# A bidirectional scan layer on one core: a main loop of hand-written order against four ordered lists, with half of a small product replaced

## The chip, the cores and the metric

The kernel runs on one core of a Trainium2 chip. The metric is device time in microseconds of that core; lower is better. The engines are called as the profile calls them: PE (TensorE, matrix products; PEld is its weight load), DVE (VectorE), ACT (ScalarE), POOL (GpSimd) and SP (SyncE, which here only issues DMAs). Each engine takes its instructions in order and waits on semaphores for the others. PE writes to PSUM, which has eight banks of 512 f32 columns on 128 partitions; POOL does not touch PSUM in this kernel.

## What is computed

Four images of 128 channels by 96 x 96 are normalised in groups, read as sequences in four directions (rows, rows reversed, columns, columns reversed), each run through the same small recurrent layer, and fused back into the image. Cut to what matters, with `x` a sequence of length 9216:

```python
t = grouped1x1(x, in_proj_w, in_proj_b, 4)          # 128 -> 512 channels
u, gate = t[:, :256], t[:, 256:]
u = depthwise_conv(silu(u), dw_w)                   # 5 taps along the sequence
s = ssm_in_w @ u                                    # 32 channels
a = clip(0.999 + 0.0009 * sigmoid(delta_w @ u + delta_b))
b, c = tanh(b_w @ u + b_b), tanh(c_w @ u + c_b)
h = scan(h' = a * h + b * s)                        # written with cumulative sums in the reference
u = u + ssm_out_w @ (c * h + d * s)
y = out_proj_w @ grouped1x1(u * sigmoid(gate), mix_w, mix_b, 4) + out_proj_b
out = x + sum over the directions of fuse_w[direction] @ y + fuse_b
```

Everything is f32.

## The kernel before, in words

The sequence is cut into steps of 16 image lines (6 steps for a pass), and a step's 1536 positions into four residues modulo 4, `p` = 0 to 3, so that a tile has 384 columns. A forward sequence and its reverse are handled together as `s` = 0 and 1: one **pair** is one residue of one step for both. There are 4 images x 2 orders (columns "V", rows "H") x 6 steps x 4 residues = 192 pairs; 24 pairs make a phase (one image, one order). In the second half of a phase the two sequences have met: the data of a step are those of a mirrored earlier step, so its silu values and gates are not computed again but loaded back from DRAM, where they had been stored (`kept_sil`, `kept`).

For each pair the work is, with the names of the tiles:

- **front** (first half of a phase only, four pairs ahead): input projection `psum<-x_in,wn` on PE (L134), silu on ACT (L481) into `sil`. Channels 0 to 127 (block 0) are laid out so that partitions hold 32 channels of four neighbouring residues, channels 128 to 255 (block 1) one residue each.
- **convolution**: block 1 by five taps, the first on ACT (L624), four on DVE (L626), the last of which writes `u`. Block 0 on PE: a product with the banded matrix `band` (128 rows, 8 matmuls) in `conv`, and in `conv_less` one with a half-band matrix `less` (64 rows, 8 matmuls) for the taps that reach into the neighbouring group of four residues. ACT copies the sum to `u` (L607, L609).
- **projections** `psum<-u,main` (16 matmuls), tanh and copies on ACT (L655 to L657, L669), decay and b*s on POOL (L659, L660).
- **scan** on DVE (L686), in two halves once in four pairs, and on POOL c*h, + d*s and a copy (L692 to L694).
- **gates**: `psum<-x_in,wn` from four matmuls (L492) and four tanh on ACT (L515), first half only.
- **state out** `psum<-t,main` (L498, four matmuls), added to `u` by an earlier copy of `u` into the bank on ACT (L506, `under`), or by a DVE add (L574) where the pair is one of the first; then the gating on DVE (L575).
- **result** `psum<-u,w_fin` (16 matmuls), copied by ACT (L717, L719) and added to the image `acc` in SBUF by POOL (L733). After the last pairs of an image `acc` is stored to `out` and reloaded with the next image.
- for the V order, statistics of the next image by `bn_stats` on DVE (L398).

A matmul of f32 shows as two entries in the profile, so the 16 matmuls of a projection are "x32".

What sets the order: `pair(t)` emits all of this for slot `t`, engine by engine in the order of its statements, with the later stages of the pair `t - 6` (`LAG`). The scheduler is off (`manual_schedule`), so each engine's queue is this order. Banks are fixed by hand (`SSM`, `TAPS`, `PROJ`, `FRONT`, `GATE`). `late` postpones the adds of an image's first pairs until its reload; `tail` drains the last six pairs, with half of the adds on DVE. All loads and stores are issued by SP in the same order.

Of the kernel before, what the change touches and what calls it, by code (L numbers as in the profile page):

```python
# [61 lines left out]
LAG = 6  # L62
UB = 8
NP = NS * R


@with_exitstack
def conv_preact_kernel(
# [28 lines left out]
    for ph, (b, order, dirs) in enumerate(phases):  # L97
        for st in range(NS):
            for p in range(R):
                for s in range(2):  # L100
# [10 lines left out]
                            "k": 2 * p + s,  # L111
# [9 lines left out]
    SSM, TAPS, PROJ = 0, 0, (4, 5)  # L121
    FRONT = (7, 6, 2, 3)
    GATE = {True: (6, 4, 5, 7), False: (4, 7, 6, 5)}

    def plan(with_front):

        return (PROJ, FRONT[:2]) if with_front else (FRONT[:2], PROJ)

# [40 lines left out]
    stats, free = {}, [FRONT[1]]  # L169
# [134 lines left out]
    d_sb, b_mix, b_out, b_fuse = (w_small[:, a:b] for a, b in ((79, 80), (80, 82), (82, 83), (83, 84)))  # L304
    w_out = w_out_fuse[:, 0:HID]
# [21 lines left out]
    less = wp.tile([P, R, 4, 32], F32, name="less")  # L327
# [8 lines left out]
    for s in range(2):  # L336
        for p in range(R):
            for k in range(2):
                r, to = slice(0, P), band[:, s, p]
                if k == less_of(p):  # L340
                    r, to = less_rows(s, p), less[:, p]
# [41 lines left out]
    def chunks_of(t):  # L383

        un = units[2 * t]
        b, k = un["b"] + 1, t % R
        if un["order"] == "V" and b < B and k > 1:
            return [(b, un["st"] * R + 2 * (k - 2) + e) for e in range(2)]
        return []

    def load_chunks(t):
        for b, c in chunks_of(t):
            chunks[b, c] = wk.tile([P, SC], F32, tag="xs", name=f"xs_{b}_{c}")
            nc.sync.dma_start(chunks[b, c], xr[b, :, bass.ts(c, SC)])

    def stats_chunks(t):
        for b, c in chunks_of(t):
            nc.vector.bn_stats(stats_of(b)[:, c, :], chunks.pop((b, c)))  # L398


    sils = {}
# [3 lines left out]
            [  # L405
                dp.tile([P, 2, 2, N + 1], F32, tag=f"sil{e}_{st}_{g}", name=f"sil{e}_{st}_{g}")
                for g in range(R)
            ]
            for st in range(NS // 2 - 1)
# [4 lines left out]
    def front(i, banks):  # L414
        for _ in front_parts(i, banks):
            pass

    def front_parts(i, banks):

        step, g = divmod(i, R)  # L420
        if step * UB >= NU:
# [7 lines left out]
        elif g == 0 and fresh(step):  # L429
            sils[step] = wk.tile([P, 2, 2, 4, N + 1], F32, tag="sil", name=f"sil_{step}")  # L430
        if fresh(step):
            yield from compute_front(step, g, banks)
        sil = sils[step]

        if st == 0:
            engine = nc.gpsimd if step else nc.vector
            for s in range(2):
                engine.memset(sil[64 * s : 64 * s + 64, s, 0, g, 0:1], 0.0)
            if g < 2:
                engine.memset(sil[:, :, 1, g, 0:1], 0.0)  # L440

# [5 lines left out]
        if st < NS // 2 - 1:  # L447
            to_keep.append((step, g))
        if step > 1:
            keep_silu(1)  # L450

    to_keep = []

    def keep_silu(n):
        for step, g in to_keep[:n]:
            nc.sync.dma_start(kept_sil[step // NS % 2][step % NS][g], sils[step][:, :, :, g, :])
        del to_keep[:n]

    def load_silu(step, gs):
        if 0 in gs:  # L460
            sils[step] = wk.tile([P, 2, 2, 4, N + 1], F32, tag="sil", name=f"sil_{step}")
        for g in gs:
            nc.sync.dma_start(
                sils[step][:, :, :, g, :], kept_sil[step // NS % 2][NS - 1 - step % NS][g]
            )

    def compute_front(step, g, banks):
        un = units[step * UB]
        wn, bn = stats[un["b"]]
        sil = sils[step]  # L470
        for s in range(2):
# [518 lines left out]
```

## Time and profile before

| | |
|---|---|
| median of 3 runs | 1841.06 us (1839.93 to 1841.37) |
| span of the profiled execution | 1839.2 us |
| granted PE clock, mean | 0.991 |
| instructions | 57257 |
| DMA traffic | 321.18 MB, mean 175 GB/s |

The profile comes from one execution, whose own time is the span. In it a line like `L134 PE MATMUL psum<-u,main ... x6144 | 534.9, 489 | 0.0` is a group of instructions: source line, engine, operation, output and inputs by the program's names, count, then busy time of the group in us, mean ns of one, and idle time of the engine ahead of them with what ended it. L134 is the helper that all 32-column matmuls go through, so they are told apart by their tiles. In a timeline line the first number is the start in us and the second the length of a run of like instructions. Matmuls are pipelined: the busy time of neighbours overlaps, and the distance of two starts is what a product costs.

### The profile page before, as it was taken

The numbers are of one execution on the slowest core, as the hardware profiler recorded it, in microseconds if no ns is written. First come the engines' busy times: TensorE is split into PE (matmuls) and PEld (weight loads), VectorE is DVE, ScalarE is ACT, GpSimd is POOL, SyncE is SP. The second block draws the span as 40 slices with busy tenths as digits, with TensorE's granted clock in tenths as the row PEclk, the third lists the DMA queues.
The fourth block names the chain that finished last, engine by engine and source line by source line (L and its number), as shares of the span: only waits on it lengthen the run. The fifth ranks groups of instructions, "written<-read, shape, count | busy, mean of one in ns | idle before, by whom it ended". The sixth has DMA issues, their size and how long they took to land.

```text
span 1839.2 us, 57257 instructions
## 1 busy us (share of the span) xinstructions
PE 1803.0 (98%) x24024; PEld 648.3 (35%) x24024; DVE 1447.5 (79%) x1444; ACT 1568.9 (85%) x2773; POOL 1446.7 (79%) x1520
## 2 busy tenths in 40 slices
PE   6999999999999999999999999999999999999997
PEld 3233333333333333333333333333333333333332
DVE  5788878877778888877787888877877778778885
ACT  4888888988888888898888888888888888888975
POOL 5478887878777888787877888787877788887786
PEclk7999999999999999999999999999999999999998
DMA  6655463443965566244695556443476634635434
GB/s 195 192 196 178 140 196 117 171 144 130 296 239 178 168 181 209 100 143 139 202 300 203 167 168 209 135 148 114 161 238 222 230 130 149 194 102 178 147 116 161
DMA packets 147825, 321.18 MB, mean 175 GB/s; under 512 B 14192, under 2 KB 115696, under 8 KB 147568
## 3 DMA queue, kind: packets, MB, share of 16 engines
q1 hardware_dynamic: 147136, 316.56, 52.8%
q8 instruction: 189, 3.10, 0.7%
q10 hardware_dynamic: 432, 0.96, 0.1%
q14 instruction: 68, 0.56, 0.1%
HBM read 185.21 MB, written 132.25 MB: 173 GB/s over the span
## 4 chain that ended last, share of the span: by engine, by line
PE 93%; ACT 3%; POOL 2%; DVE 1%; issue 0%; POOLq 0%; DVEq 0%; ACTq 0%
PE psum L134 80%; PE psum L498 8%; PE psum L492 5%; ACT sil L481 1%; ACT psum L624 0%; ACT u L607 0%; POOL t L693 0%; ACT t L657 0%; POOL acc L733 0%; POOL t L692 0%; ACT t L669 0%; ACT tm L655 0%; ACT t L656 0%; POOL t L659 0%; POOL t L694 0%
## 5 line engine op out<-in xcount | busy, mean ns | idle before, releaser
L626 DVE SCALAR_TENSOR_TENSOR psum<-sil,small,psum 128x768 f32<-128x768 f32 x576 | 588.9, 1022 | 38.8 <-ACT psum L624 13.3
L575 DVE SCALAR_TENSOR_TENSOR u<-gate,psum 128x768 f32<-128x768 f32 x376 | 349.6, 952 | 258.3 <-ACT gate L515 118.4
L134 PE MATMUL psum<-u,w_fin 128*32 128x384 f32 x6144 | 552.8, 489 | 0.0
L134 PE MATMUL psum<-u,main 128*32 128x384 f32 x6144 | 534.9, 489 | 0.0
L733 POOL TENSOR_TENSOR acc<-ys,acc 128x384 f32<-128x384 f32 x376 | 414.2, 1122 | 29.2 <-ACT ys L719 8.5
L692 POOL TENSOR_TENSOR t<-t,t 64x384 f32<-64x384 f32 x192 | 236.5, 1232 | 158.1 <-PE psum L492 78.8
L134 PEld LDWEIGHTS psum<-u,w_fin 128*32 128x32 f32 x6144 | 188.3, 110 | 321.8 <-issue 220.5
L134 PEld LDWEIGHTS psum<-u,main 128*32 128x32 f32 x6144 | 181.7, 109 | 326.0 <-issue 198.6
L134 PE MATMUL psum<-sil,band 128*32 128x384 f32 x3072 | 288.7, 490 | 8.1 <-ACT ys L719 3.1
L506 ACT COPY psum<-u 128x768 f32<-128x768 f32 x352 | 276.8, 800 | 14.0 <-DVE u L626 8.9
L659 POOL TENSOR_SCALAR t<-tm 64x384 f32<-64x384 f32 x191 | 176.9, 926 | 140.5 <-ACT tm L655 104.2
L693 POOL TENSOR_TENSOR t<-t,t 64x384 f32<-64x384 f32 x192 | 249.1, 1297 | 15.1
L498 PE MATMUL psum<-t,main 32*128 32x384 f32 x1536 | 240.6, 514 | 4.5 <-POOL t L693 2.2
L624 ACT ACTIVATE psum<-sil,small 128x768 f32<-128x768 f32 x192 | 174.1, 907 | 60.5 <-DVE u L575 53.6
L515 ACT ACTIVATE gate<-psum,bnorm 128x384 f32<-128x384 f32 x384 | 192.6, 582 | 28.7 <-PE psum L492 26.6
L660 POOL TENSOR_TENSOR t<-t,tm 64x384 f32<-64x384 f32 x192 | 195.0, 1015 | 15.8 <-ACT t L656 0.5
L626 DVE SCALAR_TENSOR_TENSOR u<-sil,small,psum 128x768 f32<-128x768 f32 x192 | 194.9, 1015 | 7.8
L481 ACT ACTIVATE sil<-psum,bnorm 128x385 f32<-128x385 f32 x384 | 191.6, 584 | 5.4 <-POOL band L344 3.3
L134 PE MATMUL psum<-sil,less 64*32 64x384 f32 x3072 | 168.8, 497 | 0.0
L492 PE MATMUL psum<-x_in,wn 32*128 32x384 f32 x768 | 162.2, 528 | 2.3 <-ACT u L607 1.2
L719 ACT COPY ys<-psum 128x384 f32<-128x384 f32 x287 | 132.8, 476 | 32.6 <-PE psum L134 32.0
L134 PEld LDWEIGHTS psum<-sil,band 128*32 128x32 f32 x3072 | 89.3, 109 | 183.7 <-issue 90.4
(84 smaller groups left out, 1506.0 us busy)
## 6 DMA issues: line engine op xcount, KB each, us to landing
sil<-sil SPq DMA_DIRECT2D x128, 770.0 KB, 6.7
kept<-gate SPq DMA_DIRECT2D x80, 768.0 KB, 3.7
gate<-kept SPq DMA_DIRECT2D x76, 768.0 KB, 5.1
x_in<-in_xs SPq DMA_DIRECT2D x192, 96.2 KB, 2.4
out<-acc SPq DMA_DIRECT2D x48, 384.0 KB, 7.8
acc<-in_xr SPq DMA_DIRECT2D x38, 384.0 KB, 6.6
xs<-in_xr SPq DMA_DIRECT2D x72, 192.0 KB, 4.6
x_in<-in_xs SPq DMA_DIRECT2D x184, 48.1 KB, 3.7
```

The lines of the kernel that those rows point to most:

```text
L134: nc.tensor.matmul(o[r, : rhs.shape[-1]], lhsT, rhs, start=start, stop=stop, skip_group_check=True)
L481: nc.scalar.activation(sil[:, s, j, g, :], bank(banks[2 * s + j])[:, : N + 1], AF.Silu, bias=bn[:, 1:2] if j else bn[:, 4 + g : 5 + g],)
L492: nc.tensor.matmul(bank(to)[:, :N], stats[un["b"]][0][r, s, :], x_in[s][r, q, off : off + N], start=True, stop=True)
L498: nc.tensor.matmul(bank(SSM + 2 * s + j)[:, :N], w_so[r, bass.ts(j, P)], z[r, :], start=bi not in seeded, stop=True, skip_group_check=True)
L506: nc.scalar.copy(psum[:, SSM + 2 * s : SSM + 2 * s + 2, :N], us[bi][:, s])
L515: nc.scalar.activation(gv[:, s, j, :], bank(to[2 * s + j])[:, :N], AF.Tanh, bias=bn[:, 2 + j : 3 + j], scale=0.5,)
L575: nc.vector.scalar_tensor_tensor(v, g, 1.0, pz, ALU.add, ALU.mult)
L626: nc.vector.scalar_tensor_tensor(us[i][:, :, 1, :] if k == K - 1 else part, src, w_tap[:, k : k + 1], part, ALU.mult, ALU.add,)
L660: nc.gpsimd.tensor_mul(ta[0:64, p, :], tb[0:64, :], tm[0:64, :])
L692: nc.gpsimd.tensor_mul(ta[0:64, p, :], tb[64:P, :], ta[64:P, p, :])
L693: nc.gpsimd.tensor_add(tb[0:64, :], ta[0:64, p, :], tb[0:64, :])
L733: adder.tensor_add(part, y, part)
```

## The change

1. **No half-band product for residues 0 and 3.** `EDGES = {0: (0, 1, 0), 3: (3, 0, 1)}`. For those two residues the `less` matrix held a single tap (the first or the last of five). Its eight matmuls and the ACT copy of the sum go; instead DVE multiplies that tap's input by a per-partition weight and adds the `band` sum from PSUM, writing `u` (`edge_tap`, "E"). The input has to have the partitions of the output, 32 channels of all four residues, so it is read from the silu values in DRAM: `load_edge` ("LE") issues two DMAs of 128 x 384 a pair into one buffer. For that, the silu tiles of all three first-half steps are stored, not of two, in a layout with the residue group inside.
2. **Four ordered lists.** `pair` and `tail` are replaced by `slot(t)`, which goes through one of four lists of named operations (by `slot_kind`: `front`, `both` fronts and gates, `gate`, `none`). `LAGS` gives for each name how many slots behind (or, negative, ahead) it works: T0 to T4 are the taps, C0/C1 `band`, L `less`, UC the copy to `u`, P0a/P0b/P1a/P1b the projections in halves (a in the pair's slot, b in the next), TM/SC/CT/SS ACT's part, DEC/BS POOL's, SCAN0/SCAN1, CH/ADD/CP, UND0/UND1 (`under`) or AU0/AU1 (the DVE add), S.. state out, G.. gates with TH0 to TH3, GAT0/GAT1 the gating, W.. the result, YS0/YS1, ACC0/ACC1, F.. fronts with SIL0 to SIL3, BN statistics.
3. **Rented banks.** A bank is taken when the first of a tenant's operations is emitted and given back after its last (`rent`, `TENANTS`), by preference (`BANKS`) or the longest free.
4. **Held adds.** An add is held in a list until all of its image's reloads are emitted; the first is then emitted at the start of slot 56 of each two phases, right behind the four reloads.
5. The residues run in the order 1, 0, 3, 2. Statistics chunks come in one load of 768 columns. The results' buffers are one for each side. The tail is nine more slots, with CP on ACT for the last four pairs and all adds on POOL.

```diff
+PLAN = {
+    "front": """
+        T1 F1 F3 CP YS1 TM F2 F0 DEC P1b T2 P0b W01 AU0 SIL1 SIL3 SIL0 W00 SC BS T3 T4 SIL2 ZERO
+        UND1 SCAN0 UND0 AU1 YS0 G00 C0 C1 S11 CT SS S00 ACC0 ACC1 S10 G01 SCAN1 S01 CH BN G10 E
+        TH0 G11 L W10 W11 PIECE GAT0 TH1 UC P0a GAT1 ADD TH2 P1a T0 TH3
+    """,
...
+    "gate": """
+        P0b YS1 CP AU1 P1b ACC1 T1 TM T2 AU0 UND1 C1 DEC CT C0 SC W00 L T3 SS T4 UND0 W01 BS S11
+        E SCAN1 S10 G00 CH UC YS0 S00 G01 G11 TH0 BN S01 ACC0 G10 SCAN0 TH1 GAT1 W11 PIECE W10
+        ADD P1a T0 P0a TH3 GAT0 TH2
+    """,
...
+}
+LAGS = {
+    "F0": -4, "F1": -4, "F2": -4, "F3": -4, "SIL0": -4, "SIL1": -4, "SIL2": -4, "SIL3": -4,
+    "T0": -1, "P1b": 1, "P0b": 1, "TM": 1, "SC": 1, "CT": 1, "DEC": 1, "BS": 1, "SCAN0": 4,
+    "SCAN1": 5, "SS": 2, "CH": 5, "ADD": 5, "CP": 6, "UND0": 6, "UND1": 6, "S00": 6, "S01": 6,
+    "S10": 6, "S11": 6, "G00": 6, "G01": 6, "G10": 5, "G11": 5, "TH0": 6, "TH1": 6, "TH2": 5,
+    "TH3": 5, "AU0": 6, "GAT0": 6, "AU1": 6, "GAT1": 6, "W00": 7, "W01": 7, "W10": 7, "W11":
+    7, "YS0": 7, "YS1": 8, "ACC0": 7, "ACC1": 8
+}
...
+MOVES = {
+    "front": "LS XG KG XC LF KS LE SEND LK",
+    "both": "LS XC LF KS LE XG SEND LK KG",
+    "gate": "LF LS KS LE XC XG SEND LK KG",
+    "none": "LF LS KS XG KG LE XC LK SEND",
+}
+TBUFS, YBUFS, HOLD = 6, 1, ()
+ORDER = (1, 0, 3, 2)
+EDGES = {0: (0, 1, 0), 3: (3, 0, 1)}
...
+    def slot_kind(t):
+
+        k = t % NP
+        if k < NP // 4 or k >= NP - R:
+            return "front"
+        if k < NP // 4 + 2:
+            return "both"
+        return "gate" if k < NP - 6 else "none"
...
+    def rent(ten, kind):
+        wide = ten in ("TB", "CB", "SS0", "SS1")
+        want = BANKS[kind].get(ten)
+        spots = [b for b in range(0, 8, 1 + wide) if not any(held_banks[b : b + 1 + wide])]
+        if want in spots:
+            b = want
+        elif wide:
+            b = min(spots, key=lambda x: max(released[x : x + 2]))
+        else:
+            b = min(spots, key=lambda x: (not held_banks[x ^ 1], released[x]))
...
+    def load_edge(n):
+        if n >= NPAIR or not edged(n):
+            return
+        un = pair_of(n)
+        step = un["step"]
+        q, k, _ = EDGES[un["p"]]
+        t = edges[n] = wk.tile([P, 2, N], F32, tag="edge", bufs=1, name=f"edge_{n}")
+        a = k if fresh(step) else 1 - k
+        for s in range(2):
+            e = s if fresh(step) else 1 - s
+            kept_rows = kept_of(step)[R - 1 - q if s else q].rearrange("g h s j n -> (g h) s j n")
+            nc.sync.dma_start(t[:, s, :], kept_rows[:, e, 0, a : a + N])
+
+    def edge_tap(n, frm):
+        un = pair_of(n)
+        t, w = edges.pop(n), EDGES[un["p"]][2]
+        nc.vector.scalar_tensor_tensor(
+            u_of(n)[:, :, 0, :],
+            t if fresh(un["step"]) else t[:, :, ::-1],
+            w_edge[:, w : w + 1],
+            two(frm),
+            ALU.mult,
+            ALU.add,
+        )
...
+    def release(kind):
+        while held and loaded[pair_of(held[0][1])["b"]] == 2 * NS:
+            emit(*held.pop(0), kind)
...
+    def slot(t):
+        if len(reload) == 4 and (t % R == 1 or t % (2 * NP) == 8):
+            load_next()
+        kind = slot_kind(t)
+        release(kind)
+        due = False
+        for op in PLAN[kind].split():
+            n = t - LAGS.get(op, 0)
...
+            elif op[:3] == "ACC" and 0 <= n < NPAIR:
+                held.append((op, n))
+                release(kind)
+            else:
+                emit(op, n, kind)
...
+        for move in MOVES[kind].split():
+            MOVE[move](t)
...
-        for t in range(NU // 2):
-            pair(t)
-        tail()
+        for t in range(NPAIR + 9):
+            slot(t)
+        send()
```

An operation is emitted only where `active` says so: L and UC for residues 1 and 2, E for 0 and 3, the F, SIL, G and TH operations for the first half of a phase, SCAN0 and SCAN1 for every fourth pair.

775 lines of the change are left out of this document (399 added, 376 removed).

## The prediction

> **What bounds the kernel now.** I read the page first: the span, the busy line, the slices and the shares of the chain that ended last.
>
> ```profile
> span 1839.2 us, 57257 instructions
> PE 1803.0 (98%) x24024; PEld 648.3 (35%) x24024; DVE 1447.5 (79%) x1444; ACT 1568.9 (85%) x2773; POOL 1446.7 (79%) x1520
> ...
> PE   6999999999999999999999999999999999999997
> ...
> PEclk7999999999999999999999999999999999999998
> ...
> PE 93%; ACT 3%; POOL 2%; DVE 1%; issue 0%; POOLq 0%; DVEq 0%; ACTq 0%
> ```
>
> TensorE is busy from the second slice to the last but one, at the full granted clock, and the chain that ended last runs through it for 93%. A busy PE need not be a PE that can go no faster, so the next view is its timeline: the start of one product to the start of the next is what the product costs. First come the first and the last start of the `band` product (the 192 pairs have one each), then a stretch with gates, then one without.
>
> ```profile
> 35.02 3.62 PE L134 MATMUL psum<-sil,band 128*32 128x384 f32 x16 [1.81 <-ACT sil L481]
> ...
> 143.84 1.47 PE L134 MATMUL psum<-sil,band 128*32 128x384 f32 x16
> 145.13 1.47 PE L134 MATMUL psum<-u,w_fin 128*32 128x384 f32 x16
> 146.53 0.88 PE L134 MATMUL psum<-sil,less 64*32 64x384 f32 x16
> 147.33 1.50 PE L134 MATMUL psum<-u,w_fin 128*32 128x384 f32 x16
> 148.76 0.59 PE L492 MATMUL psum<-x_in,wn 32*128 32x384 f32 x2
> ...
> 152.95 1.47 PE L134 MATMUL psum<-sil,band 128*32 128x384 f32 x16
> ...
> 1785.91 2.76 PE L134 MATMUL psum<-u,w_fin 128*32 128x384 f32 x32
> 1788.61 0.88 PE L134 MATMUL psum<-sil,less 64*32 64x384 f32 x16
> 1789.41 0.93 PE L498 MATMUL psum<-t,main 32*128 32x384 f32 x8
> ...
> 1792.88 1.47 PE L134 MATMUL psum<-sil,band 128*32 128x384 f32 x16
> ```
>
> A pair with gates takes 152.95 - 143.84 = 9.11 us. Over all 192 it is (1792.88 - 35.02)/191 = 9.20 us. Ahead of the first product lie 35.0 us, behind the last start 46.3 us. The half-band product `less` has its own place in the queue: 147.33 - 146.53 = 0.80 us in one stretch and 0.80 us (1789.41 - 1788.61) in the other. It is not hidden beside another product.
>
> The third view is the busy time of each engine in a stretch as long as 24 pairs.
>
> ```profile
> 209.20:432.40 223.20, 222.74 (x3024) 79.97 (x3016) 180.28 (x177) 195.18 (x345) 180.22 (x193) 1.00 0.48 154
> ```
>
> Its columns after the length are PE, weight loads, DVE, ACT and POOL busy, clock, DMA share, GB/s. PE lacks 0.46 us of 223.20: it is the bound of every stage. Per pair DVE has 180.28/24 = 7.51 us, ACT 8.13, POOL 7.51, of 9.30.
>
> **The change part by part.** 1. *The removed product.* Two of four residues (96 of 192 pairs) lose `less`. The groups of both sides of the exchange:
>
> ```profile
> L134 PE MATMUL psum<-sil,less 64*32 64x384 f32 x3072 | 168.8, 497 | 0.0
> L626 DVE SCALAR_TENSOR_TENSOR u<-sil,small,psum 128x768 f32<-128x768 f32 x192 | 194.9, 1015 | 7.8
> L609 ACT COPY u<-psum 128x768 f32<-128x768 f32 x100 | 79.9, 799 | 20.4 <-PE psum L134 20.1
> L575 DVE SCALAR_TENSOR_TENSOR u<-gate,psum 128x768 f32<-128x768 f32 x376 | 349.6, 952 | 258.3 <-ACT gate L515 118.4 <-ACT u L607 101.8 <-PE psum L498 34.2
> L686 DVE TENSOR_TENSOR_SCAN t<-t 64x768 f32<-64x768 f32 x56 | 104.6, 1869 | 2.0 <-POOL t L660 0.2
> L686 DVE TENSOR_TENSOR_SCAN t<-t,t 64x768 f32<-64x768 f32 x40 | 102.3, 2558 | 1.3
> ```
>
> Half of the 168.8 us is 84.4 us off PE, 0.88 a pair. From below: the start-to-start cost, 96 x 0.80 = 76.8. From above: where `less` stood between the two halves of `w_fin`, both halves and `less` took 148.76 - 145.13 = 3.63 us, and `w_fin` in one piece takes 1788.61 - 1785.91 = 2.70: 0.93, times 96 = 89.3. I take the middle, 84.4.
>
> 2. *What replaces it.* The end tap becomes one DVE instruction with the shape of the L626 row that writes `u`, 1.015 us, which is also the copy out of PSUM, so the 0.80 us ACT copy of those pairs goes. DVE gets 96 x 1.015 = 97.4 us, ACT loses 96 x 0.80 = 76.8. Per pair, averaged: PE (223.2 - 12 x 0.88)/24 = 8.86, DVE 7.51 + 0.51 = 8.02 (91%), ACT 8.13 - 0.40 = 7.73 (87%), POOL 7.51 (85%). PE stays the longest, by 0.8 us a slot: the cover is thinner, but there.
>
> 3. *Single slots.* The average hides one. Residues run in the order 1, 0, 3, 2; 0 and 3 are the edged ones, so slots with t%4 of 1 and 2. SCAN1 also falls on t%4 = 1. There DVE has four taps, the edge, two gatings and half a scan: 5 x 1.015 + 2 x 0.952 + (1.87 + 2.56)/2 = 9.2 us, against 9.11 - 0.80 = 8.3 for PE in a gate slot. The slot before has 8.2 against 9.1, the two after 7.0 and 6.0 (plus 1.1 with statistics) against 8.3 and 9.1; the four together 30.4 to 32.6 against 34.8. DVE can run ahead by its 0.9 us in the slot before, since the gate list lets its T1 start when ACT has done T0. What it can't carry over, PE pays where a bank that GAT1 or T0 frees is wanted at the next slot's start (P0b, F3). I take 0.2 us for each of the 48 groups of four, about 9 us; bounds 0 and 0.9 x 48 = 43.
>
> 4. *Lists, lags and rented banks.* I added up the durations before each operation on its own engine, slot by slot, and followed the code's own choice of banks. The rows of the gate list's checks:
>
> ```profile
> L506 ACT COPY psum<-u 128x768 f32<-128x768 f32 x352 | 276.8, 800 | 14.0 <-DVE u L626 8.9 <-DVE u L575 2.3
> L515 ACT ACTIVATE gate<-psum,bnorm 128x384 f32<-128x384 f32 x384 | 192.6, 582 | 28.7 <-PE psum L492 26.6 <-PE psum L498 1.1
> L719 ACT COPY ys<-psum 128x384 f32<-128x384 f32 x287 | 132.8, 476 | 32.6 <-PE psum L134 32.0 <-POOL t L660 0.2 <-issue 0.2
> L669 ACT ACTIVATE t<-t,small 64x384 f32<-64x384 f32 x192 | 118.4, 617 | 3.1 <-POOL t L660 0.5
> L657 ACT ACTIVATE t<-psum,small 64x384 f32<-64x384 f32 x192 | 110.6, 576 | 4.8
> L655 ACT ACTIVATE tm<-psum,small 128x384 f32<-128x384 f32 x192 | 110.1, 573 | 16.9 <-PE psum L134 6.9
> L656 ACT COPY t<-psum 64x384 f32<-64x384 f32 x192 | 90.6, 472 | 7.3 <-PE psum L134 0.3
> L694 POOL COPY t<-t 64x384 f32<-64x384 f32 x188 | 138.3, 736 | 11.9
> ```
> ```profile
> 141.23 2.79 PE L134 MATMUL psum<-u,main 128*32 128x384 f32 x32
> ```
>
> G01 rents a bank that the copy UC frees. On ACT stand YS1, TM, UND1, CT, SC, SS, UND0, UC: 0.48 + 0.57 + 0.79 + 0.58 + 0.47 + 0.62 + 0.79 + 0.80 = 5.1 us (276.8/352 = 0.79, and busy over count likewise). On PE stand half a projection, (143.84 - 141.23)/2 = 1.3, `band` 1.3, half of `w_fin` 1.35, `less` 0.8 and four of the eight state and gate products, (150.34 - 148.76)/8 = 0.2 each (150.34 is 9.11 after 141.23): 5.6. In the same way W11 wants TH0's bank (5.1 + YS0 0.5 + TH0 0.5 = 6.1 against 6.4), and P1a TH1's (6.6 against 7.8). They are met by some tenths if the engines' slots start together. So the lists cost nothing beyond part 3; those tenths are all the cover. On the other side, slots in which PE waited before (fronts beside gates) come out more even: of the (9.20 - 9.11) x 191 = 17 us by which the mean pair is over a gate pair I take 8 as gained, bounds 0 and 12.
>
> 5. *Edge loads.* 192 DMAs of 192 KB on SP, and 96 silu stores where there were 64. Their nearest rows:
>
> ```profile
> DMA packets 147825, 321.18 MB, mean 175 GB/s; under 512 B 14192, under 2 KB 115696, under 8 KB 147568
> ...
> sil<-sil SPq DMA_DIRECT2D x128, 770.0 KB, 6.7
> ...
> out<-acc SPq DMA_DIRECT2D x48, 384.0 KB, 7.8
> acc<-in_xr SPq DMA_DIRECT2D x38, 384.0 KB, 6.6
> xs<-in_xr SPq DMA_DIRECT2D x72, 192.0 KB, 4.6
> ```
>
> There is one edge buffer: the second edged pair's loads start only when the first pair's edge tap is done, and its own tap is due about 7 us later (end of one tap to the start of the next in the list), with some 1.5 us to spare before P0a. Two loads like `xs` take about 5 us (4.6 and the second's issue). So nothing is paid; the bad end is in the rivals. The Trainium skill, "DMA: Bandwidth & Descriptors", section "Anatomy of one DMA", fits 2.0 us plus bytes over 436 GB/s; by that these loads would be there in about 3 us, an estimate. The rows measure over four, and I go by the rows. Nothing else in the sum depends on it. Traffic grows by 192 x 192 KB and 32 x 770 KB, 62 MB on 321: the DMA share of 0.48 in the stretch above becomes about 0.6.
>
> 6. *Held adds.* At the three batch changes the first add of the new batch is emitted at the start of slot 56, ahead of CP, which S11 waits for. Before, those adds stood behind DEC and BS:
>
> ```profile
> 530.55 1.01 POOL L733 TENSOR_TENSOR acc<-ys,acc 128x384 f32<-128x384 f32 x1 [0.68 <-ACT ys L719]
> ...
> 544.69 2.40 POOL L733 TENSOR_TENSOR acc<-ys,acc 128x384 f32<-128x384 f32 x2
> ```
>
> From the end of the old batch's last add (531.6) to the new one's start are 13 us, mostly store and reload. In the new list the last add ends near 5.5 us of slot 55 (10 us long), half of the stores are already out, so the reload is there about 11.5 us later, 7 us into slot 56; then add 1.1, CP 0.7: S11, due at 4.7, starts near 9. About 4 us three times, 12 us; bounds 0 and 3 x 10.
>
> 7. *End.* DVE no longer takes half of the tail's adds; POOL's list per pair there is CH, ADD and two adds. I take +2 us on the 46.3; bounds -5 and +10.
>
> **The sum**, against the profiled execution: 1839.2 - 84.4 + 9 - 8 + 12 + 2 = 1769.8. The median, 1841.06, lies 1.9 above that span, which is part of the uncertainty; I say 1770.
>
> **The rivals.**
> *Edge loads late (slower than before).* Place: E of the second edged pair. In front slots SP sends a 770 KB store just before the edge loads. If the loads queue behind it they land after 6.7 + 4.6 = 11.3 us, against 7 + 1.5: 2.8 us late, PE waits at P0a. In all 48 groups that is 134 us: 1770 + 134 = 1904. It decides from 71/48 = 1.5 us a group. For it: one buffer, one queue. Against: gate slots have no such store, and the DMA share is half. The loads also read what a silu store has written. The Trainium skill, the same page, "Two DMAs through the same engine are not ordered", says that such a reader must wait for the store's completion; that store (6.7 us) is issued a slot earlier, so by that rule only the first pair's load would wait, and it has a slot more. Chance 0.14.
> *DVE becomes the pace in its long slot.* None of the 0.9 us is carried over: 1770 - 9 + 43 = 1804, and with the batch changes at their bad end 1822. For it: 91% of DVE in order, few tenths between bank owners. Chance 0.14.
> *PE simply full.* Part 1 at its upper end, parts 3 and 6 at nothing, part 4 at 12: 1839.2 - 89.3 - 12 + 2 = 1740. For it: PE's 222.74 of 223.20 before. Against: a held add must stop POOL. Chance 0.05.
> *The product was free*, so no change: 1841. Against: the 0.80 us between starts. Chance 0.01.
>
> **How the numbers follow.** The forecast's case, 1770, has 0.66, with its own range 1748 to 1798. The 8-in-10 range takes the second rival in up to 1822 and starts at 1748, leaving out the slower rival, some of the fuller case. A difference of 0.2% (3.7 us) is about what a measurement of this kernel can tell from no change. Faster: 0.66 + 0.14 + 0.05 = 0.85; the same 0.01; slower 0.14.
>
> **What would show it.** `less` at half its count with about 84 us; PE busy near 1718 us and 97% of the span; the start of `band` to the next, 8.3 us in edged gate slots and 9.1 in others; the waits of PE on DVE below 20 us in total; a gap of about 4 us in PE about 7 us behind the reloads of `acc`. The prediction is wrong if the waits list has DVE's edge tap waiting for the edge DMA for tens of microseconds, or if the edged slots last over 9 us.

## The result, and the profile after

The changed kernel takes 2525.18 us (median; 2517.83 to 2535.43), against 1840.57 us for the kernel before on the same chip: a ratio of 1.3726, 95% interval 1.3691 to 1.3761. I had said 1770 us, faster. It is slower by 685 us.

The page of the changed kernel, profiled execution, with the same lines as were shown of the kernel before:

```profile
span 2526.4 us, 54639 instructions
PE 1993.9 (79%) x22488; PEld 685.0 (27%) x22488; DVE 1519.0 (60%) x1531; ACT 1501.1 (59%) x2586; POOL 1403.9 (56%) x1513
...
PE   5589778987777877896877787889686797888876
...
PEclk7789889898888989898988898899898897988988
DMA  5444354534656445443465545544356543544342
...
DMA 43%; PE 30%; SPq 9%; DVE 7%; issue 4%; ACT 4%; POOL 2%; DVEq 0%; POOLq 0%; ACTq 0%
```

No engine is near full, TensorE has holes in nearly every slice, and the chain that ended last runs through DMAs for 43% where it ran through PE for 93%. Yet the DMA engines are busy only to three to six tenths in nearly all slices: what is waited for is single transfers, not the bandwidth of all 16 engines. PE is busy 191 us longer than before (1803.0) although it has 1536 matmul entries (768 matmuls) fewer. That looks like a contradiction, but the granted clock has fallen too, from 0.991 to 0.876 in the mean, a factor of 1.13, and an entry of the projections has grown by 1.12, as the next lines show.

The groups of the changed kernel are the projection, the rest of the half-band product, and the edge tap with the idle time of DVE ahead of it.

```profile
L180 PE MATMUL psum<-u,main 128*32 128x384 f32 x6144 | 647.3, 547 | 231.7 <-DVE u L673 203.0
...
L180 PE MATMUL psum<-sil,less 64*32 64x384 f32 x1536 | 84.7, 498 | 0.0
...
L673 DVE SCALAR_TENSOR_TENSOR u<-edge,small,psum 128x768 f32<-128x768 f32 x96 | 97.2, 1013 | 495.0 <-DMA edge<-sil 462.6
```

The product is halved to 84.7 us and the edge taps cost DVE 97.2 us: both are what was forecast. But DVE stood idle for 495 us before those taps, 462.6 of them for the edge DMA, and the projections behind them for 232. An entry of theirs takes 547 ns, 489 before.

The chain of waits of the changed kernel, in order of time (start, length, what), a front stretch of the first phase:

```profile
47.67 24.88 DMA sil<-sil
...
72.70 0.46 SPq L668
...
73.21 9.28 DMA edge<-sil
...
82.61 1.01 DVE u L673
...
84.89 9.22 DMA edge<-sil
...
94.23 1.03 DVE u L673
95.30 4.73 PE psum L180 x49
```

The first line is the last of the first four silu stores, which lands 24.88 us after SP begins to issue it. Only then does SP issue the edge loads that read what it wrote, which take 9.28 us; then comes the tap, which frees the one edge buffer, and the second edged pair's loads take 9.22 us more. Before, stores of the same 770 KB landed after 5.8 us in the median (6.7 for stores and loads together). The 24.88 us are the longest of the 22 silu transfers on the whole chain; the shortest has 12.8, the median is 14.8. And SP itself was held in issuing that store:

```profile
47.67 8.53 SPq L620 DMA_DIRECT2D sil<-sil  x1
```

Why they are slow stands in the windows of this stretch. Columns after the length: PE, PEld, DVE, ACT, POOL busy, clock, DMA share, GB/s.

```profile
66.00:70.00 4.00, 0.00 (x0) 0.00 (x0) 0.00 (x0) 0.00 (x0) 0.00 (x0) 0.50 0.27 91
```

While the stores run and everything waits for them, the 16 DMA engines are busy to 0.27, which is the work of about four, and 91 GB/s is moved. At that rate one store of 770 KB takes 8.7 us and three take 26 (an estimate from these two numbers). SP had issued three between 43.03 and 56.2, so the 24.88 us are the time of a line of stores, and not of one. The kernel before, in the window in which its first silu store (issued at 42.1) runs:

```profile
42.00:46.00 4.00, 3.47 (x40) 0.93 (x32) 3.89 (x4) 3.15 (x7) 1.53 (x2) 1.00 0.65 222
```

The change had put the kept silu values into a DRAM tile `[4, R, 32, 2, 2, N + 1]`, so that the store's DRAM side has an outermost dimension of 4, where it had been 128 rows. The Trainium skill, "DMA: Bandwidth & Descriptors", section "Why a DMA increments its semaphore by 16 and not by 1", says that a DMA is spread over the largest number of engines, at most 16, that divides the outermost dimension (the slowest of size over 1) of both sides; the rules at the end of the page say the same as a warning. By that rule these stores and loads run on four engines; the share of 0.27 agrees. The clock of 0.50 in the same row agrees with what "TensorE: Matmul & The Clock Gate", Part 1, states of an idle TensorE, a clock of 4/8.

SP itself is held as well. Of the edge loads of the changed kernel, the time that SP took to issue each (least, median, most, in ns):

```profile
L668 SPq DMA_DIRECT2D edge<-sil x192: 315/852/12022, 72.7 to 2449.6; - x192
```

The longest issue is held 12.0 us, from 542.4 to 554.5, while earlier silu transfers are running (DMA share 0.27 to 0.30 there), and all loads behind it on SP wait with it.

### The profile page after: what moved, and what is told of

The parts are those of the page before. It is cut to its first block, busy times and chain, and to the rows that moved or that the text cites. A ratio compares the mean times of both kernels' runs of the same rounds, so it can differ in the third digit from the quotient of the medians.

```text
span 2526.4 us, 54639 instructions
## 1 busy us (share of the span) xinstructions
PE 1993.9 (79%) x22488; PEld 685.0 (27%) x22488; DVE 1519.0 (60%) x1531; ACT 1501.1 (59%) x2586; POOL 1403.9 (56%) x1513
## 4 chain that ended last, share of the span: by engine, by line
DMA 43%; PE 30%; SPq 9%; DVE 7%; issue 4%; ACT 4%; POOL 2%; DVEq 0%; POOLq 0%; ACTq 0%
PE psum L180 25%; DMA edge<-sil 20%; DMA sil<-sil 14%; SPq L668 7%; PE psum L771 3%; DMA kept<-gate 2%; DMA xs<-in_xr 2%; DVE psum L692 2%; PE psum L777 2%; DMA out<-acc 2%; DVE u L673 2%; DMA x_in<-in_xs 2%; DVE u L824 2%; DMA acc<-in_xr 1%; SPq L594 1%
## 5 line engine op out<-in xcount | busy, mean ns | idle before, releaser
L180 PE MATMUL psum<-u,main 128*32 128x384 f32 x6144 | 647.3, 547 | 231.7 <-DVE u L673 203.0
L180 PE MATMUL psum<-u,w_fin 128*32 128x384 f32 x6144 | 635.2, 528 | 41.6 <-DVE u L673 40.7
L869 POOL TENSOR_TENSOR acc<-ys,acc 128x384 f32<-128x384 f32 x384 | 446.1, 1170 | 331.0 <-ACT ys L837 167.8
L771 PE MATMUL psum<-t,main 32*128 32x384 f32 x1536 | 302.2, 564 | 155.4 <-ACT psum L767 83.0
L673 DVE SCALAR_TENSOR_TENSOR u<-edge,small,psum 128x768 f32<-128x768 f32 x96 | 97.2, 1013 | 495.0 <-DMA edge<-sil 462.6
L756 POOL TENSOR_TENSOR t<-t,t 64x384 f32<-64x384 f32 x192 | 233.0, 1213 | 169.9 <-DVE t L750 150.3
L180 PE MATMUL psum<-sil,band 128*32 128x384 f32 x3072 | 299.6, 509 | 14.8 <-DVE u L824 10.6
L783 ACT ACTIVATE gate<-psum,bnorm 128x384 f32<-128x384 f32 x384 | 211.8, 575 | 148.3 <-issue 49.2
L760 POOL TENSOR_TENSOR t<-t,t 64x384 f32<-64x384 f32 x192 | 231.9, 1208 | 7.5
L777 PE MATMUL psum<-x_in,wn 32*128 32x384 f32 x768 | 214.1, 556 | 18.5 <-DVE u L673 18.2
L708 ACT ACTIVATE tm<-psum,small 128x384 f32<-128x384 f32 x192 | 112.3, 585 | 138.3 <-PE psum L180 136.2
L771 PEld LDWEIGHTS psum<-t,main 32*128 32x128 f32 x1536 | 112.7, 193 | 299.9 <-ACT psum L767 100.7
```

What stands on the lines that cost most here:

```text
L180: nc.tensor.matmul(o[r, : rhs.shape[-1]], lhsT, rhs, start=start, stop=stop, skip_group_check=True)
L756: nc.gpsimd.tensor_mul(ta[0:64, p, :], tbs[n][64:P, :], ta[64:P, p, :])
L760: nc.gpsimd.tensor_add(z, scans[n // R][0:64, pair_of(n)["p"], :], z)
L771: nc.tensor.matmul(bank(to)[:, :N], w_so[r, bass.ts(j, P)], tbs[n][r, :], start=not seeded(n), stop=True, skip_group_check=True)
L777: nc.tensor.matmul(bank(to)[:, :N], stats[pair_of(n)["b"]][0][r, s, :], x_in[s][r, q, off : off + N], start=True, stop=True)
L783: nc.scalar.activation(gates[n % 2][:, s, j, :], bank(frm)[:, :N], AF.Tanh, bias=bn[:, 2 + j : 3 + j], scale=0.5,)
```

## Experiments

**The layout.** Theory A: a DMA with four rows outermost runs on four engines, and this alone makes the loss. Rivals: the edge loads are late whatever the stores do, or the lists, banks and held adds lose the time. The first kernel keeps the layout and cuts each store and load into four DMAs, each with 32 rows outermost (the store is shown):

```diff
-            nc.sync.dma_start(kept_of(step)[:, g], sils[step][:, :, :, g, :])
+            for c in range(4):
+                r = slice(32 * c, 32 * c + 32)
+                nc.sync.dma_start(kept_of(step)[c, g], sils[step][r, :, :, g, :])
```

> Each silu store and each silu load is cut into four DMAs of 32 partitions; nothing else changes. Theory A (a silu store whose DRAM side begins with a dimension of four runs on a quarter of the DMA engines, lands after 18 to 25 us instead of 6, and the edge loads wait for it): stores land in under 10 us, DVE's wait for the edge DMA falls from 463 us to under 50, the time to 1760 to 1820. Theory B (one edge buffer and a place behind the store in the queue, however the store is spread): the wait stays over 200 us, the time over 2000. Theory C (the lists and the rented banks are the loss, the edge only shows it): over 2200.

Measured: 1927.57 us, ratio 1.0475 (1.0457 to 1.0492). Its DMA issues and DVE's wait for the edge:

```profile
sil<-sil SPq DMA_DIRECT2D x640, 192.5 KB, 5.1
...
edge<-sil SPq DMA_DIRECT2D x192, 192.0 KB, 4.8
```
```profile
DVE u L677 <- DMA edge<-sil: 35.8, 20, 6.8
```

Of the 685 us, 597.6 are gone. The layout is the main cause, but the kernel is still slower than before, where theory A had it faster.

**Layout and edge loads apart.** Two kernels without edge loads, with the stores of the change and with the split ones:

```diff
...
-            nc.sync.dma_start(t[:, s, :], kept_rows[:, e, 0, a : a + N])
+        edges[n] = flat_edge
...
```

> The edge loads are left out; the edge tap multiplies a constant tile, so the output is not the layer's. The stores stay as in the change. A: no wait for edges, but slow silu loads in the second halves still hold up PE: 1780 to 1950. B: everything gone, 1760 to 1790. C: over 2100.

> No edge loads (constant tile, so the output is not the layer's) and the silu stores and loads in four parts: the lists, banks and held adds alone, with the product removed. A and B: the prediction's sum, 1750 to 1790. C: over 1900.

Measured: 2327.34 us (ratio 1.2641) and 1893.52 us (1.0285, 1.0264 to 1.0305). With the slow stores and loads of silu the edge loads cost 2525.2 - 2327.3 = 198 us, with split ones 1927.6 - 1893.5 = 34 us. The slow ones cost 434 us with no edge load to wait for them. And with neither, the kernel is still 52 us slower than before: a third loss, not seen so far. For the first of the two, theory A had 1950 us at most, and the time lies in the range of theory C. The second lies in no range: above the 1790 us of A and B, and below the 1900 of C.

**The layout in the kernel before.** The same DRAM tile, and nothing else, in the old kernel:

```diff
-            [
-                dp.tile([P, 2, 2, N + 1], F32, tag=f"sil{e}_{st}_{g}", name=f"sil{e}_{st}_{g}")
-                for g in range(R)
-            ]
+            dp.tile([4, R, 32, 2, 2, N + 1], F32, tag=f"sil{e}_{st}", name=f"sil{e}_{st}")
...
```

> The kernel before with only the DRAM layout of the kept silu values changed to that of the change (block of four outermost), stores and loads in one DMA each as before. A: the silu stores land in about 18 us instead of 6 with a DMA share near 0.25 where they are alone; the kernel before has nobody waiting for a store soon, but its silu loads become slow too, so the time is 1841 to 1950. B and C: landing times as before, 1841 plus or minus 5.

Measured: 2158.46 us, ratio 1.1724 (1.1690 to 1.1757), +317 us from the layout alone (the tile, and the index of its stores and loads), far over theory A's range. Its waits show how it spreads:

```profile
DVE bn L398 <- DMA xs<-in_xr: 195.5, 30, 18.5
...
DVE u L572 <- DMA gate<-kept: 91.1, 14, 14.5
PEld psum L134 <- DMA x_in<-in_xs: 75.5, 17, 17.8
```

None of the three is a silu transfer. They are loads issued by SP in the same order, which come up to 18.5 us late behind the silu transfers.

**The removed product alone.** The old kernel, half-band product of residues 0 and 3 left out and nothing in its place:

```diff
-        for g in range(4):
+        for g in range(0 if p in (0, 3) else 4):
...
```

> The kernel before with the half-band product of residues 0 and 3 left out and nothing in its place (one of five taps is missing, so the output is not the layer's). It prices the removed product by itself. If PE was the bound in every stage and the product stood in its queue at 0.80 to 0.93 us, 96 of them: 77 to 89 us less, 1752 to 1764. If ACT or DVE take over at once: 1790 to 1835. If it was hidden: 1841.

Measured: 1813.24 us, ratio 0.9852 (0.9832 to 0.9872): -27.5 us, a third of the 84.4 that I had put on it, and inside the 1790 to 1835 that were expected if ACT or DVE took over at once. PE's busy time fell by 44 us only (1758.7). One edged slot and the one behind it, PE's timeline of this kernel:

```profile
350.88 1.47 PE L134 MATMUL psum<-sil,band 128*32 128x384 f32 x16
352.17 2.76 PE L134 MATMUL psum<-u,w_fin 128*32 128x384 f32 x32
354.86 0.82 PE L492 MATMUL psum<-x_in,wn 32*128 32x384 f32 x2
355.10 0.58 PE L498 MATMUL psum<-t,main 32*128 32x384 f32 x1
...
355.80 0.85 PE L498 MATMUL psum<-t,main 32*128 32x384 f32 x4
...
357.04 2.79 PE L134 MATMUL psum<-u,main 128*32 128x384 f32 x32
359.65 1.47 PE L134 MATMUL psum<-sil,band 128*32 128x384 f32 x16
...
364.57 0.59 PE L492 MATMUL psum<-x_in,wn 32*128 32x384 f32 x2
364.59 0.58 PE L498 MATMUL psum<-t,main 32*128 32x384 f32 x1
...
366.15 2.79 PE L134 MATMUL psum<-u,main 128*32 128x384 f32 x32
368.76 1.47 PE L134 MATMUL psum<-sil,band 128*32 128x384 f32 x16
```

The edged slot takes 359.65 - 350.88 = 8.77 us, the other 9.11: the product's 0.8 us has left 0.34. The eight gate and state products take 357.04 - 354.86 = 2.18 us in the edged slot and 366.15 - 364.57 = 1.58 in the other. In the edged slot the first state product starts 0.24 us behind the first gate product, in the other beside it. So PE arrives there earlier and gives most of it back, without showing as idle. What it meets there is ACT, whose timeline in the edged slot has

```profile
354.25 0.79 ACT L609 COPY u<-psum 128x768 f32<-128x768 f32 x1
354.93 0.81 ACT L506 COPY psum<-u 128x768 f32<-128x768 f32 x1
```

From 353.77 to 359.5 ACT works without a gap, and PE follows its copies: they end at 355.04, 355.74 (`under`, which the state products add to) and 356.15 (L719), and PE's next products start at 355.10, 355.80 and 356.20. In the other slot the same three copies end 0.4 to 0.5 us before PE comes to these products. The chain through this kernel agrees: PE has 79% of it (93% before) and ACT 12% (3%). So in this stretch ACT takes over; the other stretches were not looked at in this way.

**The order of work.** Is it the lists that bring the edge loads too late? Two kernels in the old order, with the tap on DVE in the place of the product (called `conv_less` there): one with the old layout and eight edge DMAs a pair, one with the new layout and split stores, and two.

```diff
+        if p in EDGES:
+            t, w = edges.pop(i // 2), EDGES[p][2]
+            nc.vector.scalar_tensor_tensor(
+                us[i][:, :, 0, :],
...
+        load_edge(t + 1)
```

> Part 1 of the change alone, in the order of the kernel before: residues in the order 1, 0, 3, 2, the half-band product of residues 0 and 3 replaced by the DVE edge tap, silu stored for three steps in before's own layout (one DMA of 512 rows), each edge load in eight DMAs of 32 partitions, one buffer, asked for a slot ahead. If the layout was the loss and the lists gave nothing: 1765 to 1815, with DVE's wait for the edge below 30 us. If edge loads in one buffer are late in any order: over 1860, with that wait over 100 us.

> As the run before, but with the change's DRAM layout, stores and silu loads cut into four DMAs of 32 partitions, and the edge load in two DMAs of 128 rows. Same mechanism, fewer edge DMAs, more store DMAs: within 15 us of the run before, so 1765 to 1815. Over 1860 if a late edge is a matter of the one buffer.

Measured: 2095.54 us (ratio 1.1386, 1.1369 to 1.1403) and 2043.35 us (1.1098, 1.1080 to 1.1117). Both lie over 1860, on the side on which the edge loads are late in any order. DVE's taps wait 81.6 us for the edge DMA in the first kernel, less than the 100 that went with this side, and 122.0 in the second. That does not fill the 230 us by which the second lies over the run with the product left out (1813.24). So the edge loads were taken out here too:

```diff
...
-            nc.sync.dma_start(t[:, s, :], rows[:, e, 0, a : a + N])
+            edges[n] = flat_edge
...
```

> This kernel is the old order of work with the edge tap on VectorE and the split stores, and no edge loads: the tap reads a tile of a constant, so that the edge term is wrong and everything else is done. It differs from the run with the old order and split stores (2043) by the edge loads alone, and from the run that only left the half-band product out (1813) by the tap on VectorE in place of the copy on ScalarE and by the third silu store. Theory A (the edge loads come late into their one buffer, in any order): most of the distance goes, 1805 to 1865. Rival (the tap stalls VectorE by its place in the old order, whatever feeds it): over 1930, with waits of the tap on TensorE in place of those on the DMA.

Measured: 1946.29 us, ratio 1.0576 (1.0559 to 1.0593). That is in the rival's range. The tap in the old order, together with the new order of residues, the split transfers and the third silu store, costs 133 us over the run without it, and the edge loads 97 more. Starts of `band` in this kernel, and DVE between two of them:

```profile
150.34 1.47 PE L136 MATMUL psum<-sil,band 128*32 128x384 f32 x16
159.45 1.47 PE L136 MATMUL psum<-sil,band 128*32 128x384 f32 x16
172.12 1.46 PE L136 MATMUL psum<-sil,band 128*32 128x384 f32 x16
```
```profile
163.45 1.81 DVE L713 TENSOR_TENSOR_SCAN t<-t 64x768 f32<-64x768 f32 x1
165.30 1.02 DVE L618 SCALAR_TENSOR_TENSOR u<-flat_edge,small,psum 128x768 f32<-128x768 f32 x1
169.24 0.96 DVE L583 SCALAR_TENSOR_TENSOR u<-gate,psum 128x768 f32<-128x768 f32 x1 [2.93 <-PE psum L506]
```

Where the scan stands before the tap, this slot takes 12.67 us instead of 9.11. There are three such slots in each phase, 24 in all with 10.7 to 14.3 us by the starts of `band`, and together they are 82 us longer than 24 times 9.11. So the tap's place explains the larger part of the 133 us; the rest was not taken apart. The waits were not quite as the rival had them: DVE stands behind the tap, at the gating that waits for PE (L583 on PE L506, 111.5 us in all). In the lists the same work costs 1893.5: the new order is worth 53 us with this tap.

**The changes of image.** In the run with split stores and no edge loads, the starts of `band` give 221 to 224 us for the middle phases without a change of image and 235 to 237 for those with one. In the kernel before they give 223.1 to 223.3 and 223.5 to 223.8, so there a change of image costs next to nothing. Three trials follow: the first held adds later within slot 56; two result buffers, and the adds later still; no change of image at all.

```diff
-        release(kind)
+        wait[0] = t > 2 * NP and t % (2 * NP) == 8
...
+            if op == "YS0" and wait[0]:
+                wait[0] = False
+                release(kind)
```

> The split kernel with one more edit: at the three batch changes the held adds are emitted in the slot only ahead of YS0, behind CP, DEC, BS and CH, not at its start. If POOL standing in front of the reload is what makes that slot 20 to 23 us long instead of 9: each change 5 to 10 us shorter, 1897 to 1913 in all. If the reload itself is the limit: 1920 to 1930 as in the split kernel.

> This kernel is the changed one with split stores and without edge loads (1893.5; the tap reads one constant column, which frees room), with two result buffers for each side in place of one, and with the first held adds of a new image emitted one slot and a half later. Theory A (GpSimd stands in front of a reload that is on its way, and ScalarE behind it on the one result buffer): the three slots of 20 to 23 us go, and with them 25 to 42 us: 1850 to 1870. Rival (the reload is too late for these adds wherever they stand): within 8 us of 1893.

```diff
-            nc.sync.dma_start(out[b, :, r], accf[:, r])
-            if b + 1 < B:
-                reload.append((b + 1, r))
+            if b + 1 == B:
+                nc.sync.dma_start(out[b, :, r], accf[:, r])
...
```

> This kernel is the changed one with split stores and without edge loads (1893.5), and without the three changes of image in between: the image sum is neither stored nor reloaded three times, only the last one is stored, so that three of four outputs are left out. Theory A (two thirds of what the lists lose stands at the three changes of image, where the first held add stops GpSimd until the reload has landed): 1893.5 minus three times 12 to 15 us, 1848 to 1858, with all six middle phases within 3 us of 222. Rival (the lists are slower all along, and the change of image only shows it): over 1875.

Measured: the first 1932.68 us (ratio 1.0501), against 1927.57 for the split version that it differs from: no gain. The second 1892.69 us (1.0278, 1.0251 to 1.0304): no gain over 1893.52. The third 1852.50 us (1.0057, 1.0036 to 1.0077): 41.0 us less. So the changes of image cost 41 us, as theory A of the third said, but moving the adds doesn't bring it back. The second has the time that its rival gave, but not for its reason, as its trace shows further down.

All of these carry the four-fold DMAs of the split, which hold SP too. So once more with 128 rows outermost in DRAM, one DMA for each store and load: without edge loads, with them (in four DMAs a side), and without edge loads and changes of image.

```diff
-            dp.tile([4, R, 32, 2, 2, N + 1], F32, tag=f"sil{e}_{st}", name=f"sil{e}_{st}")
+            dp.tile([R, P, 2, 2, N + 1], F32, tag=f"sil{e}_{st}", name=f"sil{e}_{st}")
...
```

> This kernel is the changed one without edge loads (the tap reads a tile of a constant, so that the edge term is wrong), in which the silu values lie in DRAM with 128 rows outermost, so that a store or a load is one DMA again in place of four. It differs from the run without edge loads and with split stores (1893.5) by the number of DMAs alone. Theory A (the change of image loses its 41 us to SyncE's queue, in which a split store holds up to 5.3 us): the slots of 20 to 23 us shrink by half or more, 1860 to 1880. Rival (the loss is the order of store, reload and held add, whatever the number of DMAs): 1888 to 1898.

> This kernel is the whole change with the same repair of the layout, 128 rows outermost and one DMA for a store, so that an edge load has to be four DMAs of 32 partitions for each side. Theory A (the count of DMAs on SyncE costs): within 20 us of the split version's 1927.6, since the DMAs that the stores save the edge loads spend again. Rival (only DMAs on few engines cost, their count does not): it comes to the run without edge loads plus what the edge loads took in the split version, 34 us or less; if that run is near 1870, below 1905.

> This kernel is the first of these three without the three changes of image in between as well (three of four outputs are left out). Theory A (what then is left is the end of the program, 14.6 us longer, and the lists' uneven slots): 1840 to 1853, against 1852.5 with split stores. Rival (the removed product shows once the DMAs are out of the way): below 1825.

Measured: 1880.83 us (ratio 1.0207, 1.0189 to 1.0224), 1930.84 us (1.0495, 1.0457 to 1.0533) and 1837.84 us (0.9986, 0.9977 to 0.9996). The count of DMAs costs 12.7 us (1893.5 to 1880.8). That is just outside theory A's range, and its mechanism isn't the one: the slots at the changes of image are still 18.6, 21.4 and 20.5 us long. The whole change, at 1930.8, is where theory A had it: what the stores save the edge loads spend again. The last is 2 us under theory A's range and 13 over the rival's. The changes of image cost 43.0 us here as well, so they belong to the change and not to the repair. The chain of the first of these three, at the first change of image:

```profile
547.19 1.45 SPq L849
548.74 5.72 DMA acc<-in_xr
...
554.71 1.16 POOL acc L866
555.92 0.51 POOL t L761
556.48 1.01 PE psum L768 x2
...
559.54 0.37 SPq L314
...
560.68 3.80 DMA kept<-gate
564.48 0.57 ACT gate L780
565.09 4.08 PE psum L180 x48
```

SP issues the reload (L849), it lands at 554.5, the held add runs, then POOL's copy (L761), and PE's state product starts at 556.5. That is part 6's mechanism. But it isn't all. SP's next load of `x_in` (L314) goes out only at 559.5, just behind PE's gate products, which read the buffer's old content; the store of the gates stands behind it on SP, ACT's next tanh (L780) waits for that store, and PE waits again to 565.1. One lateness is paid twice, the second time through SP. In the trial with two result buffers the lateness has another form. These are POOL's last add of the old image there and its first ones of the new image:

```profile
549.96 1.01 POOL L870 TENSOR_TENSOR acc<-ys,acc 128x384 f32<-128x384 f32 x1
...
575.25 5.79 POOL L870 TENSOR_TENSOR acc<-ys,acc 128x384 f32<-128x384 f32 x5
```

From the end of the one to the start of the others are 24.3 us, where the kernel before took 13. POOL is busy with another operation up to 575.2, so these adds stand where the trial's list has put them and don't wait for the reload, which SP had issued by 562.1. The slots of 20 to 23 us are gone there (the longest at the three changes have 16.6, 17.1 and 15.2 us), and yet the time is the same: the loss has moved, and is not undone. No run shows what would shorten it; the reload on another queue was not tried.

## Where the 684 us went

The runs above follow, each against the next. They come from several chips, on which the kernel before took 1840.6 to 1841.1 us; the last row is from the chip of the two rows above it:

| step | us | difference |
|---|---|---|
| the change | 2525.2 | |
| silu stores and loads split, so that each DMA has 32 rows outermost | 1927.6 | -597.6 |
| no edge loads | 1893.5 | -34.1 |
| one DMA for each store and load | 1880.8 | -12.7 |
| no changes of image | 1837.8 | -43.0 |
| the kernel before | 1841.1 | +3.3 |

The table goes in one order; the first two steps enlarge each other (434 and 198 us the other way round).

What remains of the last step, from the profile of that run: span, first and last `band`.

```profile
span 1836.1 us, 54211 instructions
```
```profile
41.19 2.79 PE L180 MATMUL psum<-sil,band 128*32 128x384 f32 x16
...
1775.43 1.50 PE L180 MATMUL psum<-sil,band 128*32 128x384 f32 x16 [0.88 <-DVE u L689]
```

Ahead of the first start 41.2 us (35.0 before), from first to last 1734.2 (1757.9, and 1731.1 in the old kernel with the product left out), behind it 60.7 (46.3). So with every disturbance taken out the main part gains 23.6 us, and the beginning and the end give 20.5 of it back. (`band` stands later in the slot in the lists than in the old order, so of beginning and end only the sum is firm.)

## Why the prediction was wrong

**Part 5 is the step that failed**: "Two loads like `xs` take about 5 us ... So nothing is paid". I took the 6.7 us row of the silu stores for stores whose DRAM side the change had rewritten, and looked at size and number, not at shape. A store of that shape takes 8.7 us even at the 91 GB/s that the four engines moved (the estimate above), and behind others 12.8 to 24.9 us were measured. DVE waited up to 26.1 us for an edge load, and other loads on SP came late as well. The slow silu transfers and the edge loads cost 631.7 us (597.6 + 34.1). What I wrote would show it is what the waits list showed, with 462.6 us. The 4.6 us of an `xs` load was a good price once the stores were right (4.8), and yet DVE waited 35.8 us for edges. The fit of the Trainium skill ("DMA: Bandwidth & Descriptors", "Anatomy of one DMA"), from which the prediction worked out about 3 us, is stated there for DMAs that GpSimd issues, and these are issued by SP. The median of these loads was 4.8 and 5.1 us in the two runs that list one of 192 KB, so the rows were the better guide.

**The first rival** had the right place, and its condition, loads that land more than 1.5 us too late, came true. Its price was 134 us; it rested on a 6.7 us store and on the 48 groups of edged pairs, and it counted only what waits for the edges, not the 434 us that the slow stores and loads cost with no edge load at all. The rule that it names, that a reader has to wait for the store's completion, agrees with the chain: SP issues the edge load at 72.70, after the store's end at 72.55.

**Part 1** was mis-sized: -84.4 forecast, with 76.8 as the lower bound, -27.5 measured by itself and -23.6 from first to last `band` in the lists. The 0.80 us between starts was the product's cost in the queue, but a queue position isn't a saving: without the product, PE's gate and state products wait for ACT's copies in the same slot, and in the gate stretch only 0.34 us of the 0.80 was left. "PE lacks 0.46 us of 223.20" hid that, since these products read as busy while they wait: eight of them take 2.18 us instead of 1.58. The same stretch had ACT busy for 195.18 of 223.20 us in the mean, and nothing was said of how close it comes in a single slot. That is also the fault in "the product was free": it was, for two thirds. In the lists ACT doesn't copy in the edged pairs, and what holds the gain to 23.6 us there was not shown.

**Part 2** was right in its price: 97.2 us for 96 taps. **Part 3** forecast 9 us for DVE's long slot. In the lists it isn't to be seen by itself: by the starts of `band` four gate slots take 36.0 us there (9.0, 8.7, 9.2, 9.2), against the 34.8 plus 0.2 that I expected. The two edged ones are the 9.0 and the 8.7, and in the old order without product and tap they take 8.7 to 8.8; so the two together are some 0.2 us longer with the tap than without. In the old order the same instruction in a bad place made slots of 12.67 us; so the second rival's mechanism is real, and the lists avoid it.

**Part 4**, that lists and rented banks cost nothing, holds about: 23.6 us gained from first to last `band` in the lists, without edge loads, changes of image and the split, against 1757.9 - 1731.1 = 26.8 in the old order with the product left out. The 8 us that I had counted on top did not come.

**Part 6** forecast 4 us for each change of image; 14.3 were measured (43.0/3). At the change that was looked at, the first wait, up to the state product, was in the forecast; the second, through SP's load of `x_in` and the gates' store behind it, was not. I had counted the reload's own path, not what its lateness does to SP's next transfers. **Part 7** forecast +2 us for the end with +10 as bound; it is +14.4, and another 6.2 at the beginning, where I had counted nothing; the two together are the 20.5 us above.

Part 5 alone doesn't account for the miss. With the silu stores and loads repaired the whole change takes 1928 to 1931 us, and with edge loads that cost nothing, as part 5 had it, still 1881 to 1894: slower than before, and outside my range, because of parts 1, 6 and 7. None of the versions with the edge loads beats the kernel before.

## What to carry to other kernels

When a change rewrites the layout of a tensor in DRAM, none of the old DMA rows prices its transfers: look at the outermost dimension of both sides, and keep it large (4 rows cost this kernel 598 us against 32). What is taken off a full engine is worth what its next wait leaves: take the product out alone before building the thing that replaces it, here -27.5 us where its busy time said -84.4. On an in-order DMA queue the price of a transfer is also paid by all that is issued behind it, so a reload or a slow store is to be followed to the other loads on that queue.

## What was not expected of the hardware

- Transfers of 770 KB with 4 rows outermost on their DRAM side ran at a DMA share of 0.27 and 91 GB/s, which is 8.7 us for one (an estimate); with others in line ahead of them, those on the chain took 12.8 to 24.9 us. Cut into four with 32 rows each, a piece landed after 5.1 us in the median, and one transfer with 128 rows after 6.2 us.
- SP was held up to 12.0 us in issuing a single DMA while earlier silu transfers were running. In the kernel before, no silu store or load took longer than 2.3 us to issue.
- The granted clock fell to 0.50 in a stretch without matmuls, and to 0.876 in the mean of the changed kernel (0.991 before), so that waiting for DMAs also made the matmuls longer: 547 ns an entry instead of 489 in the projections.
